# ScalarE instead of SyncE issues attention's plain loads from the second group of heads on

## The chip, the cores and the metric

The kernel runs on one core of a Trainium2 chip. A core has a matrix engine (TensorE, PE in the profile), three engines for elementwise work (VectorE or DVE, ScalarE or ACT, GpSimd or POOL), and SyncE (SP), which does no arithmetic here and issues transfers. Sixteen DMA engines move the data between main memory and the on-chip memory. Each engine takes its own instructions strictly in order, and the engines wait for each other by semaphores. The metric is the device time of one execution in microseconds (us): the median of the runs.

## What is computed

The input x has 1024 rows of 512 numbers. It is normalized by rows, and the result goes into two branches: causal attention with 32 query heads in 8 groups (one key head and one value head for four query heads, each 128 wide) with a linear distance bias, and a feed-forward network with 4-bit weights. The result is x plus the product of the two.

```
xn = layernorm(x)
q, k, v = xn @ Wq.T, xn @ Wk.T, xn @ Wv.T          # 32, 8 and 8 heads of 128
q, k = rmsnorm(q, q_norm_w), rmsnorm(k, k_norm_w)
scores = q @ k.T / sqrt(128) + where(j > i, -1e30, slope[head] * (j - i))
s = concat_heads(softmax(scores) @ v) @ Wo.T
g = silu((silu(xn @ gate) * (xn @ up)) @ down)     # weights (w - zero) * scale
out = x + s * g
```

## The kernel before

The feed-forward network comes first, then the projections of the query, key and value heads, and then attention. Nearly all matrix products use 16-bit numbers in pairs: a value is split into a high and a low half, and one product becomes three matmuls (`mm3`, lines 151 to 153). The feed-forward result (the gates) and the projected heads are parked in main memory: keys in `kd`, values in `vd`, queries in `qd`, gates in `gd`. Attention loads them back, a group of heads at a time.

Attention is a pipeline of 256 steps written out by hand, in `step(n)`. A group of heads has 32 steps: four blocks of 256 query rows (`qb`; from the second group on in the order 2, 3, 0, 1, in the last group 2, 3, 1, 0), and in a block four heads with two tiles of 128 query rows each. A block therefore has 8 steps. Later blocks of rows see more keys (the mask is causal), so their tiles are wider: a tile of block 3 has up to 1024 columns, a tile of block 0 128 or 256. In step n the engines are given, in this order:

- the loads that are due at its start: queries of the next block two steps after a block began, keys of the next group at step 4 of 32, values of the next group at step 24 of 32;
- PE: the scores of step n, into one of two score tiles in PSUM (`s`);
- ACT: every second step, the copy of the finished head outputs of ten steps ago (`heads_hi`, line 1110);
- DVE: the biased scores of step n-1 and their row minimum (line 1041); ACT: their exponentials and row sums (line 1047);
- ACT: the high half of the probabilities of step n-3 (line 1066); DVE: the low half of those of step n-4 (line 1074), and right behind it SP issues a DMA transpose of both halves, from `p16` into `pT` (lines 1082 and 1077);
- PE: the products of probabilities and values of step n-9 (`o`), and between them output projections of an earlier block (`m`), which DVE adds up (line 1149);
- at the step's end, in some steps: loads of gates and x for the last group (`gate_load`), and rows of Wo. Wo's row blocks are loaded at every second step (`load_wo`, line 991), scaled by GpSimd two steps later (line 994), and split into halves two more steps later (lines 1000 and 1001).

Buffers are taken from rings in turn: two slots for keys, values and queries each, four for Wo rows, four for gates, five for `p16`, four for transposed probabilities (two named `pT`, two named `wide`). A transfer into a slot waits until the slot's last reader is done.

All transfers are issued by SP. A DMA transpose goes out on the same queue as the loads, in the order of the program. The queries of the group before the last are transposed as they are loaded (line 962), and those of the last group come from on-chip memory, transposed (line 974).

The first 8 of the 256 steps run between the last projections, and `attention` runs the others. It is in the program twice, once for the case that a bound on the scores allows far keys to be skipped. The branch with the skipping is the one that the profiled execution takes.

Of the kernel before, what the change touches and what calls it, by code (L numbers as in the profile page):

```python
# [22 lines left out]
P = 128  # L23
# [4 lines left out]
NH = 4  # L28
HD = 128
# [7 lines left out]
NQT = QB // P  # L37
# [72 lines left out]
def attention_gated_by_ffn_kernel(ctx, tc, x, gu_w, gu_z, gu_s, dn_w, dn_z, dn_s, wq, wkv, wo, qnw, knw, out):  # L110
    nc = tc.nc
    ve, se, ge, te, sp = nc.vector, nc.scalar, nc.gpsimd, nc.tensor, nc.sync
# [9 lines left out]
    def ps2():  # L122
        return rings["s"].take(F32, 2, 512)
# [52 lines left out]
    kd = [dram.tile([P, 2, NT, 2 * HD], F16, name=f"kd{i}") for i in range(HKV // 2)]  # L176
    vd = [dram.tile([P, NT, 2 * HD], F16, name=f"vd{g}") for g in range(HKV)]
    qd = [dram.tile([NT, P, 2 * NH * HD], F16, name=f"qd{g}") for g in range(HKV)]
    ald = [dram.tile([1, 2 * HD], F32, name=f"ald{i}") for i in range(HKV // 2)]
    gd = dram.tile([NT, P, DM], F32, name="gd")  # L180
# [358 lines left out]
    def finish_step():  # L539

        for f in finishing.pop(clock[0], ()):
            f()
        clock[0] += 1
# [282 lines left out]
    for it in range(NI):  # L826
        for tb in range(2):
# [14 lines left out]
            for i in range(4):  # L842
                c = slice(i * P, i * P + P)
# [100 lines left out]
    NB = S // QB  # L944
    blocks = [(g, qbs) for g in range(HKV) for qbs in (FIRST_ORDER if g == 0 else ORDER if g < HKV - 1 else LAST_ORDER)]
    units = [(g, qb, hh) for g, qbs in blocks for hh in range(NH) for qb in qbs]
    kT, vT, qT, woh, wol = {}, {}, {}, {}, {}
    trel, pT, oT, wor = {}, {}, {}, {}

    def load_keys(g):  # L950
        kT[g] = rings["kT"].take(F16, NT, 2, P)
        sp.dma_start(kT[g].rearrange("p t a k -> p t (a k)"), kd[g // 2][:, g % 2])

    def load_values(g):
        vT[g] = rings["vT"].take(F16, NT, 2, HD)
        sp.dma_start(vT[g].rearrange("p t a d -> p t (a d)"), vd[g])

    def load_queries(g, qb):
        qT[g, qb] = rings["qT"].take(F16, NQT, 2, NH, P)
        if g == HKV - 2:  # L960
            for i in range(NQT):
                sp.dma_start_transpose(qT[g, qb][:, i].rearrange("p a g q -> p (a g) q"), qd[g][qb * NQT + i])
            return
        sp.dma_start(
            qT[g, qb].rearrange("p t a g q -> p t (a g q)"), qd[g][qb * NQT : (qb + 1) * NQT].rearrange("t p c -> p t c")
        )

# [2 lines left out]
    def last_queries(t):  # L970
        g, qb = HKV - 1, t // NQT
        if (g, qb) not in qT:
            qT[g, qb] = rings["qT"].take(F16, NQT, 2, NH, P)
        sp.dma_start_transpose(
            qT[g, qb][:, t % NQT].rearrange("p a g q -> p (a g) q"), last_pairs.pop(t).rearrange("p a g d -> p (a g d)")
        )
# [11 lines left out]

    def load_wo(g, i):
        wor[g, i] = rings["wor"].take(F32, DM)  # L990
        sp.dma_start(wor[g, i], wo[(g * NH + i) * HD : (g * NH + i + 1) * HD, :])

    def scale_wo(g, i):
        ge.tensor_scalar(wor[g, i], wor[g, i], rvs[:, g : g + 1], None, ALU.mult)  # L994
# [8 lines left out]
    def relative(g):  # L1003

        rel = trel[g] = rings["trel"].take(F32, S)
        if g == 0:
            ge.iota(rel, pattern=[[-1, S]], base=S - P, channel_multiplier=1, allow_small_or_imprecise_dtypes=True)
            ge.affine_select(rel, rel, pattern=[[-1, S]], compare_op=ALU.is_ge, fill=1e20, base=S - P, channel_multiplier=1)
            ge.tensor_scalar(rel, rel, rc, float(SLOPES[NH - 1]), ALU.mult, ALU.mult)
        else:  # L1010
            ge.tensor_scalar(rel, trel[g - 1], float(SLOPES[g * NH + NH - 1] / SLOPES[g * NH - 1]), None, ALU.mult)
# [8 lines left out]
    def scores(u, qt):  # L1020
        g, qb, hh = units[u]
        k0 = lowest(u, qt)
        w = (NQT * qb + qt + 1 - k0) * P
        ps = ps2().rearrange("p a c -> p (a c)")
        q = qT[g, qb][:, qt]
        for c0 in range(0, w, 512):
            c1 = min(w, c0 + 512)
            kt = kT[g][:, k0 + c0 // P : k0 + c1 // P]
            mm3(ps[:, c0:c1], (q[:, 0, hh, :], q[:, 1, hh, :]), (kt[:, :, 0, :], kt[:, :, 1, :]), True, True)
        s_ps[u, qt] = ps[:, :w]  # L1030
# [77 lines left out]
    def heads_hi(u):  # L1108
        oh, ol = rings["oh"].take(F16, QB), rings["ol"].take(F16, QB)
        se.activation(oh, av_ps[u], AF.Copy, scale=1.0 / P_SCALE)  # L1110
        oT[units[u]] = (oh, ol)

    def heads_lo(u):
        oh, ol = oT[units[u]]
        ve.scalar_tensor_tensor(ol, av_ps.pop(u), 1.0 / P_SCALE, oh, ALU.mult, ALU.subtract)  # L1115
# [12 lines left out]
    def gate_load(qb):  # L1128
        gx = rings["f"].take(F32, 2, NQT, DM)
        t0 = qb * NQT  # L1130
        sp.dma_start(gx[:, 0], gd[t0 : t0 + NQT].rearrange("t p c -> p t c"))
        sp.dma_start(gx[:, 1], x[t0 * P : (t0 + NQT) * P, :].rearrange("(t p) c -> p t c", p=P))
        gates[qb] = gx

    def gate_partial(qb, i):
# [5 lines left out]
    def accumulate(g, qb, i, other=False):  # L1141
        ps = op_ps.pop((g, qb, i))
        t = qb * NQT + i
        yt = y_rows(t)
        undo = isg[:, g : g + 1]
        if g == 0:
            ve.tensor_scalar(yt, ps, undo, None, ALU.mult)
        elif g < HKV - 1:
            ve.scalar_tensor_tensor(yt, ps, undo, yt, ALU.mult, ALU.add)
        else:  # L1150
            gt = gates[qb][:, 0, i]
            ve.scalar_tensor_tensor(gt, ps, undo, gt, ALU.mult, ALU.mult)
            (ge if other else ve).tensor_tensor(gt, gt, yt, ALU.add)
            sp.dma_start(out[t * P : (t + 1) * P, :], gt)

    order = [(u, qt) for u in range(len(units)) for qt in range(NQT)]
    nn, BS = len(order), NH * NQT
# [3 lines left out]
    for k, (g, qbs) in enumerate(blocks[:-1]):  # L1161
# [5 lines left out]
        n, taken, done = max(free, due), 0, 0  # L1167
        op_first.setdefault(g, n)
        for qb in qbs:
            for i in range(NQT):  # L1170
                for part in range(NH):
# [5 lines left out]
                    if taken == 2 or n < due + done:  # L1177
                        n, taken = n + 1, 0
        free = n + (taken > 0)
    near = [False]  # L1180
    TILES = NT * len(projections)

    def at(n):

        return order[n] if 0 <= n < nn else None
# [3 lines left out]
    def advance(stage, n):  # L1189

        while stages[stage] <= n and at(stages[stage]):
            stage(*at(stages[stage]))
            stages[stage] += 1
# [9 lines left out]
    def step(n):  # L1203
        nonlocal last_ps
        if n < nn:
            u, qt = order[n]
            g, qb, hh = units[u]
            for due in q_at.get(n, ()):
                if due[0] < HKV - 1:
                    load_queries(*due)  # L1210
            for t, due in LAST_QUERIES.items():
                if due == n:
                    last_queries(t)
            if g + 1 < HKV:
                if n % (NB * BS) == KEYS_STEP:
                    relative(g + 1)
                    load_keys(g + 1)
                elif n % (NB * BS) == VALUES_STEP:
                    load_values(g + 1)
            scores(u, qt)  # L1220
        done = at(n - AV_LAG - 1)
        done = done[0] if done and done[1] == NQT - 1 else None
        if done is not None:
            heads_hi(done)
        for stage, lag in ((biased, 1), (exponentials, 1), (split_hi, NQT + 1), (split_lo, NQT + 2)):
            advance(stage, n - lag)
        if done is not None:
            heads_lo(done)
        if n < nn + AV_LAG + 1:
            for due in acc_at.get(n, ()):  # L1230
                accumulate(*due)
        finish_step()

        def project():
            for due in op_at.get(n, ()):
                out_proj(*due)

        if at(n - AV_LAG):
            values(*at(n - AV_LAG), project)
        else:  # L1240
            project()
        if done is not None and units[done][:2] == final:
            g, qb, hh = units[done]
            if hh == 0:
                last_ps = [ps2()[:, 0, :] for i in range(NQT)]
            for i in range(NQT):
                out_proj(g, qb, i, hh)
            if hh == NH - 1:
                for due in acc_at.get(nn + AV_LAG + 1, ()):
                    accumulate(*due, other=True)  # L1250
                for i in range(NQT):
                    accumulate(g, qb, i)
        if n in GATE_LOADS:
            gate_load(LAST_ORDER[GATE_LOADS.index(n)][0])
        for i in range(NQT):
            if n - i in GATE_SUMS:
                gate_partial(LAST_ORDER[GATE_SUMS.index(n - i)][0], i)
        for lead, act in ((WO_SPLIT, split_wo), (WO_SCALE, scale_wo), (WO_LOAD, load_wo)):
            for g, first in op_first.items():
                if n + lead - first in range(0, 2 * NH, 2):  # L1260
                    act(g, (n + lead - first) // 2)
# [36 lines left out]
                early_tile(c)  # L1298

    def attention(only_near):  # L1300
        near[0] = only_near
        for k in range(len(projections) - 2, len(projections)):
            project_all(k)
        for n in range(NT, nn + AV_LAG + 1):
            step(n)

    def frozen():
# [21 lines left out]
    with tc.If(flag > 0) as branch:  # L1329
        attention(True)  # L1330
# [42 lines left out]
```

## Time and profile before

| | |
|---|---|
| median of 3 runs | 1016.7 us (1016.07 to 1020.3) |
| profiled execution | 1020.44 us, span of its instructions 1018.6 us |
| PE busy in the span | 964.7 us (95%) |
| DVE, ACT, POOL busy | 857.2 (84%), 775.5 (76%), 429.4 us (42%) |
| DMA transposes of probabilities | 224 on SP, from 446 us on |
| attention's plain loads on SP | 8 keys, 8 values, 24 queries, 32 rows of Wo, 4 of gates, 4 of x |

The profile is of one execution. A row such as `L1066 ACT ACTIVATE p<-pf,row` is line 1066 of the kernel, on ScalarE, writing the tile `p` from `pf` and `row`. `SPq` and `ACTq` are the queues of SP and ACT themselves: their rows are DMA issues and semaphore waits, which count as no engine's busy time. A DMA row's duration is the time for which the issue held the queue, not the transfer. In the lists of waits, `PE o L151 <- DMA pT<-p: 9.5, 6, 3.7` says that PE, before line 151's matmul into `o`, sat idle 9.5 us in all, in 6 places, the longest 3.7 us, until a DMA from `p` to `pT` had landed. The granted clock is the share of full speed that TensorE was given.

### The profile page before, as it was taken

To read this page: it belongs to the slowest core of one execution; us is meant where nothing else is said; L and a number is where in the kernel's file an instruction comes from. 1 tells how busy PE (TensorE), PEld (TensorE's weight loads), DVE (VectorE), ACT (ScalarE), POOL (GpSimd) and SP (SyncE) were. 2 spreads that over 40 slices of the span, in tenths; PEclk is the share of its full clock that TensorE was granted. 3 is DMA by queue.
4 is the path that set the end of the run, shared out by engine and by line. 5 is a ranking of instruction groups with operands and counts; after the bars stand their busy time and mean duration, and the time that the engine had idled before them with its cause. 6 is when DMAs were issued, how large, how long until landed. Compare 5 with 4: busy or idle time off the path is not lost. (4 is left out here: it accounts for less than half of the span.)

```text
span 1018.6 us, 17980 instructions
## 1 busy us (share of the span) xinstructions
PE 964.7 (95%) x5688; PEld 561.8 (55%) x5688; DVE 857.2 (84%) x1764; ACT 775.5 (76%) x2160; POOL 429.4 (42%) x424
## 2 busy tenths in 40 slices
PE   6899999999999999996998999999999999989995
PEld 4344477854444444444555666665676666656562
DVE  7888998728888878877898998987989989969985
ACT  5777745778878887787887987987879978858861
POOL 2588764216666555564235151051241421530722
PEclk9999999999999999999999999999999999999999
DMA  7132359535998999998898999997999999999994
GB/s 251 37 121 93 104 170 310 187 125 163 204 273 190 245 229 215 236 237 202 172 196 161 206 216 183 227 203 158 231 202 191 212 201 190 202 219 198 218 201 108
DMA packets 425063, 195.74 MB, mean 192 GB/s; under 512 B 371522, under 2 KB 382078, under 8 KB 424958
## 3 DMA queue, kind: packets, MB, share of 16 engines
q1 hardware_dynamic: 424958, 194.50, 85.5%
q8 instruction: 46, 0.75, 0.3%
q14 instruction: 59, 0.48, 0.1%
HBM read 76.27 MB, written 27.27 MB: 102 GB/s over the span
## 5 line engine op out<-in xcount | busy, mean ns | idle before, releaser
L1074 DVE SCALAR_TENSOR_TENSOR p<-pf,row,p 128x384 f16<-128x384 f32 (+7 forms) x256 | 208.8, 816 | 20.9 <-ACT p L1066 18.0
L1047 ACT ACTIVATE pf<-pf,row 128x384 f32<-128x384 f32 (+7 forms) x256 | 184.9, 723 | 41.6 <-DVE row L1041 37.3
L1041 DVE CUSTOM_DVE_ANT_0 pf<-s,trel,cs 128x384 f32<-128x384 f32 (+7 forms) x256 | 191.4, 748 | 19.8 <-PE s L153 19.7
L1066 ACT ACTIVATE p<-pf,row 128x384 f16<-128x384 f32 (+7 forms) x256 | 184.0, 719 | 6.3 <-DMA pT<-p 1.4
L151 PE MATMUL s<-kT,qT 128*128 128x512 f16 (+3 forms) x356 | 115.3, 324 | 11.8 <-DVE row L1041 11.5
L994 POOL TENSOR_SCALAR wl<-wl,rvs 128x512 f32<-128x512 f32 x32 | 53.7, 1677 | 149.0 <-DMA wl<-in_wo 130.0
L152 PE MATMUL s<-kT,qT 128*128 128x512 f16 (+3 forms) x356 | 115.4, 324 | 0.0
L153 PE MATMUL s<-kT,qT 128*128 128x512 f16 (+3 forms) x356 | 114.0, 325 | 0.0
L716 POOL TENSOR_TENSOR f<-f,inv 128x512 f32<-128x512 f32 (+1 forms) x96 | 102.1, 1084 | 1.4
L151 PE MATMUL m<-v,wh 128*128 128x512 f16 x248 | 95.0, 383 | 0.0
L153 PE MATMUL m<-v,wh 128*128 128x512 f16 x248 | 94.9, 383 | 0.0
L151 PE MATMUL o<-pT,vT 128*128 128x256 f16 (+1 forms) x302 | 79.6, 264 | 13.9 <-DMA pT<-p 13.7
L151 PEld LDWEIGHTS <-vT 128*128 128x128 f16 x594 | 58.9, 99 | 57.8 <-DMA pT<-p 15.1
L1110 ACT ACTIVATE wh<-o 128x256 f16<-128x256 f32 x128 | 47.7, 373 | 54.4 <-PE o L153 53.8
L152 PEld LDWEIGHTS <-vT 128*128 128x128 f16 x594 | 58.9, 99 | 41.4 <-issue 4.5
L152 PE MATMUL o<-pT,vT 128*128 128x256 f16 (+1 forms) x302 | 79.6, 264 | 0.0
L153 PE MATMUL o<-pT,vT 128*128 128x256 f16 (+1 forms) x302 | 79.3, 264 | 0.0
L151 PE MATMUL o<-wide,vT 128*128 128x256 f16 (+1 forms) x292 | 75.9, 260 | 3.1 <-DMA wide<-p 3.1
L152 PE MATMUL o<-wide,vT 128*128 128x256 f16 (+1 forms) x292 | 75.9, 260 | 0.0
L153 PE MATMUL o<-wide,vT 128*128 128x256 f16 (+1 forms) x292 | 75.7, 260 | 0.0
L151 PE MATMUL m<-wh,xth 128*128 128x512 f16 x192 | 72.8, 379 | 1.2 <-ACT h L869 1.2
L153 PE MATMUL m<-wh,xtl 128*128 128x512 f16 x192 | 72.8, 379 | 0.0
(200 smaller groups left out, 2531.4 us busy)
## 6 DMA issues: line engine op xcount, KB each, us to landing
qd<-tr SPq DMA_DIRECT2D x48, 256.0 KB, 3.3
qT<-qd SPq DMA_DIRECT2D x24, 512.0 KB, 4.4
wide<-in_wq SPq DMA_DIRECT2D x32, 256.0 KB, 3.7
wo_sq<-in_wo SPq DMA_DIRECT2D x8, 1024.0 KB, 7.8
wl<-in_wo SPq DMA_DIRECT2D x32, 256.0 KB, 3.6
gui<-in_gu_w SPq DMA_DIRECT2D x13, 512.0 KB, 3.7
wide<-in_wkv SPq DMA_DIRECT2D x16, 256.0 KB, 3.8
vd<-v SPq DMA_DIRECT2D x8, 512.0 KB, 4.7
```

The costliest lines, as they stand in the source:

```text
L151: te.matmul(ps, lhsT=lh, rhs=rh, start=first, stop=False)
L152: te.matmul(ps, lhsT=lh, rhs=rl, start=False, stop=False)
L153: te.matmul(ps, lhsT=ll, rhs=rh, start=False, stop=last)
L716: ge.tensor_tensor(f, f, ib, ALU.mult)
L994: ge.tensor_scalar(wor[g, i], wor[g, i], rvs[:, g : g + 1], None, ALU.mult)
L1041: ve.tensor_tensor_reduce(p, ps, trel[g][:, S - w :], cs[:, hh : hh + 1], 3e38, ALU.add, ALU.min, least[:, c])
L1047: se.activation(p, p, AF.Exp, bias=least[:, c], scale=-1.0, accum_out=total[:, c])
L1066: se.activation(p16[u, qt][:, :, 0, :], pf[u, qt], AF.Copy, scale=scale[:, qt : qt + 1])
L1074: ve.scalar_tensor_tensor(lo, p, scale, hi, ALU.mult, ALU.subtract)
L1110: se.activation(oh, av_ps[u], AF.Copy, scale=1.0 / P_SCALE)
```

## The change

From step 32 on (`NB * BS`, where the second group of heads begins), the plain loads of keys, values, queries, Wo rows, gates and x are issued by ScalarE's queue (`se`) and no longer by SyncE's (`sp`). They stand at the same places of the program, and what they load, from where and to which buffer is the same. The transposes, those of the queries among them, and the output's stores stay on SyncE. The loads of the first group's steps, up to step 31, stay there too.

```diff
+    def loads():
+        return se if loads_by_act[0] else sp
+
     def load_keys(g):
         kT[g] = rings["kT"].take(F16, NT, 2, P)
-        sp.dma_start(kT[g].rearrange("p t a k -> p t (a k)"), kd[g // 2][:, g % 2])
+        loads().dma_start(kT[g].rearrange("p t a k -> p t (a k)"), kd[g // 2][:, g % 2])
     def load_values(g):
         vT[g] = rings["vT"].take(F16, NT, 2, HD)
-        sp.dma_start(vT[g].rearrange("p t a d -> p t (a d)"), vd[g])
+        loads().dma_start(vT[g].rearrange("p t a d -> p t (a d)"), vd[g])
...
@@ load_queries, the plain form
-        sp.dma_start(
+        loads().dma_start(
             qT[g, qb].rearrange("p t a g q -> p t (a g q)"), qd[g][qb * NQT : (qb + 1) * NQT].rearrange("t p c -> p t c")
         )
...
@@ load_wo
-        sp.dma_start(wor[g, i], wo[(g * NH + i) * HD : (g * NH + i + 1) * HD, :])
+        loads().dma_start(wor[g, i], wo[(g * NH + i) * HD : (g * NH + i + 1) * HD, :])
...
@@ gate_load
-        sp.dma_start(gx[:, 0], gd[t0 : t0 + NQT].rearrange("t p c -> p t c"))
-        sp.dma_start(gx[:, 1], x[t0 * P : (t0 + NQT) * P, :].rearrange("(t p) c -> p t c", p=P))
+        loads().dma_start(gx[:, 0], gd[t0 : t0 + NQT].rearrange("t p c -> p t c"))
+        loads().dma_start(gx[:, 1], x[t0 * P : (t0 + NQT) * P, :].rearrange("(t p) c -> p t c", p=P))
...
-    near = [False]
+    near, loads_by_act = [False], [False]
...
     def attention(only_near):
-        near[0] = only_near
+        near[0], loads_by_act[0] = only_near, False
         for k in range(len(projections) - 2, len(projections)):
             project_all(k)
         for n in range(NT, nn + AV_LAG + 1):
+            loads_by_act[0] = n >= NB * BS
             step(n)
```

## The prediction, made before the change was run

> **What bounds the kernel now.** I read the waits first, cut to the stretch in which the change acts. The second group's first moved load is issued at 511 us, and the last at 989, so I ask for 515 to 1000 us: who waited, for whom, how long, how often, the longest.
>
> ```profile
> PE o L151 <- DMA pT<-p: 9.5, 6, 3.7
> PE s L151 <- DVE row L1041: 6.0, 4, 2.5
> PE o L151 <- DMA wide<-p: 3.1, 3, 2.3
> ```
>
> The matrix engine (PE) idles about 19 us in 485: 12.6 us until a DMA transpose of probabilities (pT or wide) has landed, 6.0 us until VectorE has freed a score bank. The rest is matmul work that this change leaves alone. So an improvement must come out of the transposes' lateness, and it has a ceiling. The same stretch by windows (microseconds, then busy PE, weight loads, VectorE, ScalarE, GpSimd; granted clock; DMA share; GB/s):
>
> ```profile
> 645.00:716.00 71.00, 68.97 (x476) 44.09 (x474) 61.98 (x139) 57.26 (x132) 18.61 (x14) 0.98 1.01 195
> ...
> 850.00:920.00 70.00, 64.02 (x439) 40.57 (x438) 57.16 (x125) 52.51 (x122) 22.23 (x18) 0.98 1.04 213
> 920.00:960.00 40.00, 37.91 (x245) 23.11 (x243) 39.69 (x69) 31.89 (x60) 17.21 (x10) 0.96 1.09 206
> ...
> sum 485.00, PE 465.43 PEld 297.23 DVE 434.46 ACT 391.09 POOL 151.14; mean PE 58.18 PEld 37.15 DVE 54.31 ACT 48.89 POOL 18.89
> ```
>
> ScalarE (ACT) is busy 391 of 485 us (81%), VectorE 434 (90%). ACT has 94 us free in total, but not everywhere. The DMA share near 1 warns that the transfers may be limited by the DMA engines and not by who issues them. Finer windows around one stall, same columns:
>
> ```profile
> 676.00:684.00 8.00, 8.00 (x70) 6.17 (x68) 7.65 (x21) 5.33 (x18) 3.93 (x6) 1.00 1.23 216
> 684.00:688.00 4.00, 1.97 (x18) 1.45 (x17) 2.17 (x9) 2.24 (x8) 0.31 (x1) 1.00 0.92 195
> 688.00:692.00 4.00, 4.00 (x19) 2.33 (x17) 1.08 (x4) 0.00 (x0) 0.00 (x0) 0.57 0.64 166
> ```
>
> PE loses 2.03 us idle, and in the next 4 us it is granted 0.57 of its clock: 4 x 0.43 = 1.7 us more. A stall costs nearly twice its idle time. SyncE's queue before it:
>
> ```profile
> 668.68 1.12 SPq L991 DMA_DIRECT2D wl<-in_wo  x1
> 669.90 2.98 SPq L1082 DMA_TRANSPOSE wide<-p  x1
> 672.99 4.31 SPq L1082 DMA_TRANSPOSE pT<-p  x2
> 677.39 0.72 SPq L964 DMA_DIRECT2D qT<-qd  x1
> 678.21 6.41 SPq L1082 DMA_TRANSPOSE pT<-p  x2
> ```
>
> SyncE (SP) goes from one issue to the next with 0.1 us between. The two transposes for which PE waits stand behind a query load that holds SP 0.72 us, and behind a Wo row (1.12 us). From 651.6 to 678.1 us four Wo rows and two query loads take 0.97+0.90+0.77+0.89+1.12+0.72 = 5.4 us of SP.
>
> **The change, part by part.** *What leaves SP.* Sixty-seven issues: 28 Wo rows, 19 query loads, 6 keys, 6 values, 4 gates, 4 rows of x. By their medians on SP (0.822, 0.580, 0.574, 0.575, 0.581, 0.476 us) they hold it 23.0+11.0+3.4+3.5+2.3+1.9 = 45 us; with 0.1 us between issues, 52. What remains on SP are the transposes: 84 at 1.475, 84 at 1.426, 14 at 1.241, 13 at 1.233, and 16 of queries near 1.27, so 297 us by medians, and the output stores. SP goes from some 0.72 of the stretch to 0.61.
>
> *What that is worth.* At the 684 us stall the last two transposes could start up to 0.8 us sooner (the query load), and more if SP had not lagged before. The stalls at 889 and 895 us have transposes of queries in front, which stay on SP. So I take half of the 12.6 us: 6.3. The clock row adds (1 - 0.98) x 71 + (1 - 0.98) x 70 = 2.8 us in the two windows with such stalls; half is 1.4. Gain 7.7 us; the bounds are 0 (the DMA engines set the landing) and 12.6 + 2.8 = 15.4.
>
> *What ACT takes on.* No row shows ACT issuing a DMA; its price is bounded by SP's rows, 0.40 us (shortest Wo row of the whole trace) to 1.46 (longest key load); I take SP's 0.58, nearest because the transfers are the same. That is 67 x 0.58 = 39 us of ACT's queue. How much holds up its arithmetic? One line's view in a window of 2.4 us shows ACT's queue ahead of its engine:
>
> ```profile
> L1066 ACTq EVENT_SEMAPHORE  x1: 17/17/17, 656.2 to 656.2; - x1
> L1066 ACT ACTIVATE p<-pf,row x1: 1042/1042/1042, 657.7 to 657.7; 128x896 f16<-128x896 f32 x1
> ```
>
> The queue's semaphore instruction runs at 656.2, 1.5 us before the split it belongs to, while the exponential before that split starts only at 656.49. A queue instruction thus runs once the waits ahead of it are met, not once the arithmetic ahead is done. A load is covered by arithmetic already released. The 28 Wo rows come at the end of a step, behind an exponential and a split (medians 0.721 and 0.705 us): 0.58 + 0.1 lies under 1.43, cost 0. Queries, keys and values (31) stand behind a split that waits for the row scale: 0.68 against 0.705, cost about 0. The gate pairs (4) are 0.58 + 0.48 + 0.2 = 1.26 against 0.705: 0.55 each, 2.2 us. On the path I charge 1.5, since ACT has idle time in each window. Bounds: 0, and, with nothing covered, 67 x 0.68 = 46 less whatever of the 94 us idle absorbs it.
>
> *New waits.* What is queued behind a load on ACT are the heads' copies, exponentials and splits; VectorE's low halves wait for those, SP's transposes for these, PE for the transposes. But the buffers are free by then: a query slot's last scores come three steps before the load, and ACT has already run the exponential of a later step's scores; keys four steps, values sixteen, Wo rows most of a group later. Cost 0, with that order as the cover; if an earlier DMA's landing is waited for instead, at most a landing, 3.6 us for Wo rows, beyond what ran meanwhile. GpSimd issues no DMA and only gets Wo rows earlier: its 118 us of waiting for them is idle time that nobody needs.
>
> *Sum.* -7.7 + 1.5 = -6.2 us. The profiled execution took 1020.4 us (span 1018.6 and 1.8 around it), so 1014.2 of its kind; it stands 3.7 above the median of the runs, 1016.7, so 1010.5.
>
> **Two rules against it.** The row: 297 us of transposes in 485, and a DMA share of 1.01 to 1.23. The Trainium skill (DMA: Bandwidth & Descriptors, "Issuing engines are not separate DMA queues") says that DMAs from any engine run on the same 16 engines, and that a second issuer saves only sequencer time, usually small. Taken strictly, the term of 7.7 is only SP's part: at the 684 us stall 0.8 us of 2.03. It would bring about 3 us.
> Its page Perfetto Trace Analysis, "DMA Instruction — HWDGE (DVE, Sync)", has the descriptor generator locked for exclusive use during an issue. No row here shows two issuers. If so, ACT's loads queue behind SP's transposes, and by that rule SP wins nothing; the sum becomes that of the third rival.
>
> **Rivals.** *One: hidden anyway.* For it: the DMA share, and the two transposes at 678 take 6.41 us where the two before them take 4.31: what slows an issue that far is transfers, not SP. A load of 512 KB moves over the same engines whoever issues it. Against it: the 0.1 us spacing, SP really queues. Time: 0 to -3 from freed SP time, +1.5: 1016.
>
> *Two: all late transposes catch up.* The ceiling, 15.4 us, with no ACT cost: 1001. Against it: the query transposes that remain.
>
> *Three, slower: ACT is held by SP's transposes.* Place: a load at ACT's step start that must wait until SP's running transpose is issued. SP transposes 297/485 = 61% of the time, with some 1.4 us each; a chance arrival waits 0.61 x 0.7 = 0.43 us on average, and under the long ones of 2 to 4 us far more. An issue of 1.2 us plus 0.1 exceeds the 0.705 cover by 0.6: 35 x 0.6 = 21 us of ACT, in stretches where VectorE follows ACT closely (VectorE waited 14.8 us for ACT's splits, 45 times). If half reaches PE, +10.5, with no gain: 1027. It decides once ACT's loads take over about 1.1 us at the median. For it: direct loads on SP take up to 1.46 us just behind transposes. Against it: most are near 0.58, the wait there could be SP's own queue.
>
> That the change does nothing is no rival: the branch taken uses these very lines (the loads are in the trace).
>
> **How the numbers follow.** A difference under 0.5% (5 us) is about what a measurement of this kernel can't tell from none. Forecast (-5 to -10): 0.32, point 1010.5. Hidden (within 5 us): 0.30. Full catch-up (-10 to -16): 0.08. Held ACT (above +5): 0.30. So faster 0.40, same 0.30, slower 0.30. The range runs from the ceiling, 1001, to 1027, leaving out 2 in 10, mostly above; the forecast's own range is 1006 to 1012.
>
> **What would show it.** Right: loads appear in ACT's queue at about 0.6 us, PE's waits for pT and wide fall from 12.6 toward 6 us, fewer windows show a clock below 1, ACT's waits are unchanged. Hidden: PE's waits stay, transposes on SP as long as before. Held: ACT's loads above 1.1 us, VectorE's waits for ACT's splits well above 14.8 us, PE's waits for VectorE's row above 6.0. Wrong altogether: if ACT's queue can't run ahead past a load, or if a load waits there for a buffer or an earlier DMA, each would pass its whole length on to the exponentials.

## The result and the profile after

The changed kernel takes 1026.5 us (median of 8 runs, 1023.0 to 1030.6); the kernel before takes 1017.7 us in the same comparison (8 runs, 1014.7 to 1023.6). The ratio is 1.0089, 95% interval 1.0068 to 1.0109: slower by 0.9%, or 8.8 us. The direction forecast was wrong. The profiled execution of the changed kernel took 1023.75 us (span 1022.0, mean granted clock 0.985; before 1020.44, 1018.6 and 0.989), which is 2.8 below the median of its kind, as that of before was 2.7 above. The two traces therefore differ by only 3.4 us of span, and I read them for places, not for the sum.

The waits of the changed kernel, of PE alone, from 515 to 1000 us (us in all, places, the longest):

```profile
PE o L151 <- DMA pT<-p: 15.8, 9, 4.8
PE s L151 <- DVE row L1045: 6.7, 9, 1.3
```

Before, PE waited 9.5 + 3.1 = 12.6 us for transposes; now it waits 15.8. The wait that was to shrink has grown. The wait for VectorE's row (6.0 before) is nearly as it was. From 515 to 1000 us the clock takes no more than before: the mean granted clock there is 0.987 after and 0.986 before, which is 6.3 and 6.8 us lost. The difference between the two traces in this stretch is idle time.

The issues of the moved loads, from the views of their six lines in the changed kernel (count, then shortest, median and longest ns, first and last start):

```profile
L956 ACTq DMA_DIRECT2D kT<-kd x6: 330/338/364, 515.7 to 848.9; - x6
...
L960 ACTq DMA_DIRECT2D vT<-vd x6: 333/346/393, 555.0 to 897.1; - x6
...
L968 ACTq DMA_DIRECT2D qT<-qd x19: 377/383/402, 512.6 to 815.5; - x19
...
L995 ACTq DMA_DIRECT2D wl<-in_wo x28: 334/344/399, 523.7 to 955.8; - x28
...
L1135 ACTq DMA_DIRECT2D f<-gd x4: 372/383/384, 887.6 to 988.4; - x4
...
L1136 ACTq DMA_DIRECT2D f<-in_x x4: 503/553/984, 888.0 to 988.9; - x4
```

The change does what it says, and an issue on ACT is short: 0.34 to 0.55 us by the medians of its six lines, with one of 0.98. ScalarE is busy as before (775.9 us against 775.5), and VectorE waits no longer for ACT's high halves (14.6 us against 14.8). Nobody is held up by ACT.

The page's DMA queues, after (packets, MB, share of the 16 engines' time):

```profile
q1 hardware_dynamic: 411854, 166.71, 76.0%
q10 hardware_dynamic: 13104, 27.79, 9.4%
```

and before:

```profile
q1 hardware_dynamic: 424958, 194.50, 85.5%
```

The loads have become a queue of their own, q10. The packets' time is the same in sum (85.4% against 85.5%). Last, the time from issue to landing, from the views of the tile `pT` and then of `wide` between 511 and 1000 us, before (shortest, median, longest):

```profile
DMA to landing us min/median/max: 2.7/4.1/6.3
...
DMA to landing us min/median/max: 2.7/4.0/7.7
```

and after:

```profile
DMA to landing us min/median/max: 2.7/4.4/7.4
...
DMA to landing us min/median/max: 2.8/4.1/8.8
```

So SP was relieved, and the transposes were no better off. For the 115 transposes (114 after) whose landing the traces hold from step 32 on, I took the differences of three times: the end of the low half that a transpose waits for, its issue, its landing. The mean from low half to issue fell from 1.03 to 0.81 us; the mean from issue to landing rose from 4.13 to 4.42. Together 5.16 before and 5.23 after: what was won at the issue was lost in flight. These are the transposes whose landing the views give; some slow ones, the one of 8.19 us below among them, are left out. With the last completion record of each taken as its landing, all of them in this stretch can be counted: from issue to landing 4.13 us before (197) and 4.56 after (198), and over 7 us took 1 before and 12 after.

**The place where it shows.** In the third group of heads, SP's queue before (start, us held, what):

```profile
606.01 1.61 SPq L1082 DMA_TRANSPOSE pT<-p  x1
607.72 1.03 SPq L964 DMA_DIRECT2D qT<-qd  x1
608.85 6.72 SPq L1082 DMA_TRANSPOSE pT<-p  x2
```

A transpose goes out first, then the query load of the next block (512 KB), then the next transposes. PE did not wait for any of these: from 606 to 618 us it waits only for VectorE:

```profile
PE s L151 <- DVE row L1041: 0.7, 1, 0.7
```

The same place in the changed kernel, SP's queue, then ACT's:

```profile
607.08 9.95 SPq L1086 DMA_TRANSPOSE pT<-p  x3
```

```profile
607.14 0.39 ACTq L968 DMA_DIRECT2D qT<-qd  x1
```

The load now leaves in the same instant as that first transpose, 0.06 us behind it, instead of 1.7 us. The chain of the changed kernel through this stretch (start, us, what):

```profile
606.30 0.21 PE m L151
...
607.08 8.19 DMA pT<-p
615.27 0.05 issue
615.32 0.38 PE o L151
...
617.41 0.43 PE m L151
```

The transpose takes 8.19 us to land (before, the same one, issued at 606.01, took 5.5 by its last completion record), and PE, which needs it, idles 1.5 us until it has (PE's waits from 606 to 619 us):

```profile
PE o L151 <- DMA pT<-p: 1.5, 1, 1.5
PE s L151 <- DVE row L1045: 0.7, 1, 0.7
```

The trace's packet records show the order in flight. The transposes here move packets of 256 bytes, the query load packets of 2048. Before, from 607.6 to 610.6 us, the load has been issued, but all packets under 512 bytes are the transposes', and the only other one is an instruction fetch:

```profile
DMA packets 1492, 0.40 MB, mean 133 GB/s; under 512 B 1491, under 2 KB 1491, under 8 KB 1491
```

After, from 609.0 to 610.2 us, there are packets of the load alone:

```profile
DMA packets 175, 0.36 MB, mean 299 GB/s; under 512 B 0, under 2 KB 0, under 8 KB 175
q10 hardware_dynamic: 175, 0.36, 84.4%
```

The packets of the transpose issued at 607.08 start behind them, 3.2 us after its issue; before, they had started within 1.8. The load, issued 0.06 us later than the transpose, went ahead of it.

Then the clock drops: the windows of the same kernel (us, then busy PE, weight loads, VectorE, ScalarE, GpSimd; granted clock; DMA share; GB/s):

```profile
606.00:611.00 5.00, 5.00 (x44) 3.62 (x43) 4.54 (x10) 4.87 (x13) 3.84 (x3) 1.00 0.98 221
611.00:615.40 4.40, 2.16 (x19) 1.34 (x18) 4.08 (x11) 2.65 (x12) 2.73 (x5) 1.00 1.28 139
615.40:618.80 3.40, 3.40 (x14) 1.90 (x15) 0.55 (x4) 1.09 (x4) 0.59 (x2) 0.50 1.09 243
```

For 3.4 us the granted clock is 0.50, and the matmul `m` of line 151, 0.21 us in the chain at 606.30, takes 0.43. Half of 3.4 us is another 1.7 us lost. Idle and clock make up 3.2 us, and the block of eight steps around it grew by 3.1.

### The profile page after: what moved, and what is told of

It reads as the page before. It is cut to its first block, busy times and chain, and to the rows that moved or that the text cites. A ratio compares the mean times of both kernels' runs of the same rounds, so it can differ in the third digit from the quotient of the medians.

```text
span 1022.0 us, 17989 instructions
## 1 busy us (share of the span) xinstructions
PE 965.1 (94%) x5688; PEld 562.0 (55%) x5688; DVE 857.5 (84%) x1764; ACT 775.9 (76%) x2160; POOL 428.3 (42%) x424
## 4 chain that ended last, share of the span: by engine, by line
PE 71%; DMA 9%; DVE 8%; ACT 5%; issue 4%; POOL 3%; SPq 0%; DVEq 0%; POOLq 0%; ACTq 0%
PE o L151 8%; PE o L152 8%; PE o L153 8%; PE m L151 8%; PE m L152 8%; PE m L153 8%; DMA pT<-p 7%; PE gu_ps L326 6%; PE s L151 4%; PE s L153 4%; PE s L152 4%; PE dn_ps L151 1%; PE dn_ps L153 1%; PE dn_ps L152 1%; ACT p L1070 1%
## 5 line engine op out<-in xcount | busy, mean ns | idle before, releaser
L1078 DVE SCALAR_TENSOR_TENSOR p<-pf,row,p 128x384 f16<-128x384 f32 (+7 forms) x256 | 207.1, 809 | 22.3 <-ACT p L1070 19.0
L1045 DVE CUSTOM_DVE_ANT_0 pf<-s,trel,cs 128x384 f32<-128x384 f32 (+7 forms) x256 | 191.4, 748 | 19.2 <-PE s L153 19.1
L152 PE MATMUL m<-wl,xth 128*128 128x512 f16 x192 | 72.8, 379 | 0.0
```

What stands on the lines that cost most here:

```text
L152: te.matmul(ps, lhsT=lh, rhs=rl, start=False, stop=False)
L1045: ve.tensor_tensor_reduce(p, ps, trel[g][:, S - w :], cs[:, hh : hh + 1], 3e38, ALU.add, ALU.min, least[:, c])
L1078: ve.scalar_tensor_tensor(lo, p, scale, hi, ALU.mult, ALU.subtract)
```

## The experiments

A block below is one of eight steps, from the start of its first biased scores (line 1041 before, 1045 after) to that of the next block, both from the trace. Three stretches vary with the loads and are given for every run: the third block of the third group (steps 80 to 87), the third block of the seventh group (steps 208 to 215), and the tail, from the last block's start to the end. They come from one profiled execution of each kernel, so their spread counts: in the runs that leave the loads near a stretch as before, the third group's block takes 15.7 to 16.0 us, the seventh's 22.2 to 23.5, the tail 38.9 to 40.2. The ratios come from 6 to 12 runs of each, against the kernel before on the same chip.

| run | ratio to before, 95% interval | third group | seventh group | tail |
|---|---|---|---|---|
| before | 1 | 15.8 | 23.5 | 39.1 |
| the change | 1.0089 (1.0068 to 1.0109) | 18.9 | 25.0 | 40.7 |
| tiny_on_act | 0.9995 (0.9976 to 1.0013) | 15.6 | 21.5 | 39.1 |
| wo_on_act | 0.9991 (0.9972 to 1.0010) | 15.9 | 21.8 | 39.0 |
| thin_sp | 0.9930 (0.9911 to 0.9949) | 15.6 | 19.5 | 39.2 |
| thin_act | 0.9991 (0.9974 to 1.0008) | 15.5 | 24.0 | 40.4 |
| gates_on_act | 1.0057 (1.0031 to 1.0082) | 16.0 | 23.5 | 42.0 |
| rest_on_act | 1.0047 (1.0028 to 1.0066) | 19.0 | 24.9 | 39.0 |
| first_gates_215 | 1.0109 (1.0083 to 1.0135) | 19.3 | 20.5 | 39.8 |
| gates_207_sp | 1.0024 (1.0003 to 1.0045) | 15.9 | 26.1 | 39.2 |
| queries_lead1_sp | 1.0023 (1.0005 to 1.0040) | 19.0 | 22.3 | 38.9 |
| safe_on_act | 0.9997 (0.9975 to 1.0019) | 19.2 | 17.8 | 38.8 |
| gates_early_sp | 1.0025 (1.0008 to 1.0041) | 15.8 | 23.4 | 40.2 |
| wo_gates_early_sp | 0.9998 (0.9981 to 1.0014) | 15.8 | 22.3 | 38.6 |
| one_query_on_act | 1.0032 (1.0015 to 1.0050) | 19.6 | 23.4 | 39.4 |
| values_on_act | 1.0035 (1.0019 to 1.0050) | 15.7 | 25.5 | 39.3 |
| last_gates_on_act | 1.0025 (1.0006 to 1.0044) | 15.8 | 22.2 | 41.8 |
| safer_on_act | 1.0017 (0.9995 to 1.0038) | 15.6 | 19.5 | 38.3 |

**Is it ACT?** *tiny_on_act* keeps all loads on SP and lets ACT issue 67 extra loads of 128 x 4 bytes at the same places.

```diff
+        if loads_by_act[0]:
+            se.dma_start(tiny[:, c : c + 1], x[:P, c : c + 1])
+        return sp
```

> All loads stay on SyncE; at each of the 67 places ScalarE issues in addition a load of 128 x 4 bytes into a scratch tile that nobody reads. The contention theory (loads on a second queue run beside the transposes and make them land later) expects no slowdown, because hardly a byte moves: 1016 to 1019 us against about 1017.7 before. The issue theory (each issue of 0.34 us on ScalarE's queue delays the exponentials, and they PE) expects the whole loss: about 1026 us, since the queue is held as often as in the changed kernel.

Measured 1018.6 us, ratio 0.9995. Sixty-seven issues on ACT (0.335 us in the median) cost nothing that can be measured, so the loss is not ScalarE's time.

**Is it the bytes?** *thin_sp* and *thin_act* load an eighth of the bytes of each key, value, query and Wo load, on SP and on ACT; gates and x stay whole. These two kernels leave out data, so only their times mean anything.

```diff
+        c = to.shape[-1] // 8
+        return to[..., :c], of[..., :c]
...
-        sp.dma_start(vT[g].rearrange("p t a d -> p t (a d)"), vd[g])
+        sp.dma_start(*thin(vT[g].rearrange("p t a d -> p t (a d)"), vd[g]))
```

> SyncE issues all loads, and from the second group on each load moves an eighth of its bytes (the rest of the buffer keeps older data, and Wo rows are scaled by 1 instead of the group's factor, so the result is not the reference's). Partner of the next kernel. If the loads' bytes are what makes the transposes late before the change, PE's waits for transposes fall well below 12.6 us and the time falls by 5 to 15 us; if it is SyncE's issue time, the time stays within 3 us of before.

> As the kernel before it, but ScalarE issues the loads from the second group on, as in the changed kernel. Contention theory: with an eighth of the bytes the second queue can't hurt; equal to the partner, or up to 5 us faster through SyncE's freed queue. Issue theory: slower than the partner by the same 9 us as the changed kernel against before.

Measured 1011.2 and 1018.8 us. On SP seven eighths of the bytes of these 59 loads are worth 0.7%, and PE's waits for transposes (515 to 1000 us) fall from 12.6 to 6.4 us: bytes matter before the change too. On ACT the third group's block is back at 15.5 us: a thin query load on ACT does no harm, so it is the bytes in flight beside the transpose that do. But thin_act still lost 7.6 us to thin_sp, where equal or faster was expected, with the whole gate and x loads the only large ones on ACT. That pointed at single loads, which the next runs took apart.

**Which loads?** *wo_on_act* moves the 28 Wo rows alone, *gates_on_act* the eight loads of gates and x alone, *rest_on_act* all but these eight. Each is the change with some `loads()` put back to `sp`:

```diff
 # gates_on_act: keys, values, queries and Wo back on SP
-        loads().dma_start(wor[g, i], wo[(g * NH + i) * HD : (g * NH + i + 1) * HD, :])
+        sp.dma_start(wor[g, i], wo[(g * NH + i) * HD : (g * NH + i + 1) * HD, :])
```

> Only the 28 Wo rows go to ScalarE; queries, keys, values and gates stay on SyncE. Contention theory: in proportion to bytes, 7.3 of 27.8 MB, some +2.5 us. Issue theory: in proportion to count, 28 of 67, +3.8 us, or nothing if these issues are covered by the exponential and split ahead of them, as the prediction had it.

> Only the 8 gate and x loads go to ScalarE. Overtaking theory (SyncE lags some 10 us behind ScalarE's place in the program where block 3 of a group ends; there ScalarE issues the first gate pair, 1 MB that is needed only later, ahead of transposes that PE is about to wait for): the whole loss of the changed kernel, 1024 to 1028 us, and block 0 of the seventh group 24 us or longer. General contention, in proportion to bytes: 4.2 of 27.8 MB, some +1.4 us.

> The other 59 loads (keys, values, queries, Wo rows) go to ScalarE, gates and x stay on SyncE. Overtaking theory: no loss, 1012 to 1019 us, because these loads are issued near the time at which SyncE issued them. General contention: most of the loss, some +7.6 us, 1025.

Measured 1018.2, 1025.5 and 1024.1 us. The Wo rows, 42% of the moved issues, do no harm. Eight gate and x loads cost 0.57%; in the profiled execution they lengthen the tail by 2.9 us and the third block of the eighth group from 19.1 to 21.0. The rest costs 0.47%, in the third and the seventh group, and leaves the tail alone. The two add up to 1.04%, the whole change to 0.89%, equal within the intervals. Two expectations failed here: the gates were to hold the whole loss and to lengthen the seventh group's block (it stayed at 23.5), and the rest was to cost nothing.

**Does another step cure the gates?** *first_gates_215* is the change with the first gate pair four steps later; *gates_207_sp* is the kernel before with that pair four steps earlier.

```diff
-GATE_LOADS = [211, 219, 235, 251]
+GATE_LOADS = [215, 219, 235, 251]   # first_gates_215; gates_207_sp has 207
```

> The changed kernel, with the first of the four gate pairs loaded at step 215 instead of 211, about 9 us later and so about when SyncE used to issue it. Overtaking theory: block 0 of the seventh group shrinks from 25 to 21 to 23 us, and the time by 3 to 5 us, to 1022. If the engine that issues is what costs, no change: 1026.

> The kernel before, ScalarE issues nothing; the first gate pair is moved four steps forward, to step 207, so that SyncE issues it ahead of the last four wide transposes of that block instead of behind them. Overtaking theory: the same stall as in the changed kernel without any change of engine, +3 to +6 us, 1021 to 1024. If the engine or the second queue is the cause: no change, about 1018.

Measured 1031.0 and 1021.5 us. Four steps later did not help, where 3 to 5 us less was expected: the seventh group's third block fell to 20.5 us, but its fourth rose from 14.4 to 19.7. Four steps earlier on SP put the pair ahead of more transposes, and that block became the longest of all runs, 26.1 us; the time rose by 0.24%, some 2.4 us, a little less than the 3 to 6 expected. SP gives no protection by itself; what counts is what stands behind the load.

**Order, without ACT.** *queries_lead1_sp* leaves every load on SP and issues the query loads one step sooner in their blocks, so that each stands ahead of the transpose behind which it stood.

```diff
-        for qb, lead in zip(blocks[k + 1][1], (6, 10) if steps > BS else (2, 5)):
+        for qb, lead in zip(blocks[k + 1][1], (6, 10) if steps > BS else (1, 5)):
```

> No load is on ACT here; SP issues the query loads of a group's first block one step of heads earlier than before, so that they stand ahead of the transpose behind which they stood. Order theory (a load harms when it moves beside or ahead of a transpose that PE needs next, whoever issues it): the third group's first block of queries grows from 15.8 toward 19 us with a PE stall of over 1 us in it, and the time is up by 2 to 6 us, 1020 to 1025. Engine theory (the loss belongs to ACT as issuer, or to two rings at once): no change, within 1.5 us, the block stays at 15.8.

Measured 1019.6 us, ratio 1.0023. SP's queue in this run, then its chain, then PE's own row with its idle time in brackets:

```profile
606.15 1.03 SPq L964 DMA_DIRECT2D qT<-qd  x1
607.28 7.00 SPq L1082 DMA_TRANSPOSE pT<-p  x2
```

```profile
607.28 7.63 DMA pT<-p
```

```profile
614.95 0.28 PE L151 MATMUL o<-pT,vT 128*128 128x256 f16 x1 [1.62 <-DMA pT<-p]
```

The block takes 19.0 us, as with the load on ACT (18.9 to 19.6 in the six runs where it stood beside or ahead of the transpose at its full size, counting this one), and not 15.8. From 609.0 to 610.2 us the packets are the load's alone here too (175, none under 512 bytes). The same stall comes from the order alone, with one queue and one issuer. This is what decides, at this place, between the order and the engine; for the gates gates_207_sp speaks to the same question, and for the values no run does.

**One load at a time.** *one_query_on_act* has a single load of the 67 on ACT, the query load shown above. *values_on_act* has the six value loads there, *last_gates_on_act* the last pair of gates and x.

```diff
 # one_query_on_act
-        sp.dma_start(
+        (loads() if (g, qb) == (2, 1) else sp).dma_start(
             qT[g, qb].rearrange("p t a g q -> p t (a g q)"), ...
```

```diff
 # last_gates_on_act: only gate_load uses loads(), and
+            loads_by_act[0] = n == GATE_LOADS[-1]
```

> One load of the 67 on ACT, the third group's last query load (512 KB), all else on SP. Order theory: the third group's block that holds it grows from 15.8 to about 19 us with a PE stall of 1.5 to 1.9 us, no other block differs, time up by 2 to 4 us, 1020 to 1022, ratio 1.002 to 1.004. If the loss needs the whole stream on the second ring: no change of that block, ratio within 0.0015 of 1.

> Only the six value loads (512 KB each) on ACT. Order theory: the seventh group's first block of small rows grows to 24 to 25.5 us (21.5 to 23.5 before), with a PE wait of 4.5 to 5 us for the transpose issued beside the load; the other groups unchanged, time up by 1 to 3 us, ratio 1.001 to 1.003. If values are harmless: ratio within 0.0015 of 1 and the block at most 23.5.

> Two loads on ACT, the last pair of gates and x, which go out just ahead of a late transpose of the last group. Order theory: the tail, from the last block of steps to the end, grows from 39.1 to between 40.5 and 42 us with a PE wait of over 3 us for that transpose, time up by 1.5 to 3 us, ratio 1.0015 to 1.003. If not: tail 38.9 to 39.3 and ratio within 0.001 of 1.

Measured 1.0032, 1.0035 and 1.0025, each with an interval above 1. The chain and PE's waits (608 to 620 us) of one_query_on_act:

```profile
609.74 9.11 DMA pT<-p
```

```profile
PE o L151 <- DMA pT<-p: 2.4, 1, 2.4
```

In values_on_act the value load goes out 2.2 us behind the transposes' issue, beside them; ACT's queue, the chain, and PE's waits from 880 to 920 us:

```profile
897.23 0.33 ACTq L960 DMA_DIRECT2D vT<-vd  x1
```

```profile
895.04 7.50 DMA pT<-p
```

```profile
PE o L151 <- DMA pT<-p: 7.6, 2, 6.0
```

and the same chain and waits in the kernel before, where the values wait behind four transposes, until 902.43:

```profile
893.54 5.48 DMA pT<-p
```

```profile
PE o L151 <- DMA pT<-p: 5.5, 2, 3.7
PE o L151 <- DMA wide<-p: 0.5, 1, 0.5
```

The transpose lands 7.50 us after its issue instead of 5.48, and PE's longest wait grows from 3.7 to 6.0. In last_gates_on_act, ACT's queue, SP's queue and the chain:

```profile
985.18 0.39 ACTq L1135 DMA_DIRECT2D f<-gd  x1
985.62 0.59 ACTq L1136 DMA_DIRECT2D f<-in_x  x1
```

```profile
985.99 1.23 SPq L1086 DMA_TRANSPOSE pT<-p  x1
```

```profile
985.99 7.53 DMA pT<-p
```

Here the loads leave 0.4 to 0.8 us ahead of the transpose, which takes 7.53 us, and PE waits 3.4 us for it; the tail is 41.8 us instead of 39.1. From 986.0 to 989.7 us 465 of the 466 packets are those of the loads, and the transpose's start after them. Before, the same pair went out right behind that transpose, which landed 3.1 us after its issue. Nine loads of 67 account for 0.32 + 0.35 + 0.25 = 0.92%, against 0.89% for the change. The agreement is partly luck: each term is known to about 0.2%, and the other three gate pairs (0.57 - 0.25 = 0.32%, by difference) are not in this sum. The first of them goes out in the block of the seventh group that the values burden as well, so the prices need not add.

**Can the good part be kept?** *safe_on_act* leaves on ACT the Wo rows, the keys and the queries of all blocks of rows but block 0.

```diff
-        loads().dma_start(vT[g].rearrange("p t a d -> p t (a d)"), vd[g])
+        sp.dma_start(vT[g].rearrange("p t a d -> p t (a d)"), vd[g])
...
+        (loads() if qb else sp).dma_start(
```

> On ACT from the second group on: Wo rows, keys and the queries of each block but a group's first; values, the first blocks' queries, gates and x stay on SP. Most of the moved issues, but none that my traces show in front of a late transpose. Order theory: no loss, ratio 0.997 to 1.002, third group's first block 15.8 us, seventh group's first block at most 23.5, tail 39.1. If instead any heavy load on a second ring slows transposes in proportion to its bytes: about three fifths of the loss of the whole change, +5 us, 1023.

Measured 1017.4 us, ratio 0.9997, as the order theory had it, but not for its reason. I had put the wrong query loads back: the harmful one of the third group belongs to block 1 of rows, and stayed on ACT. The chain there is as bad as in the change,

```profile
608.66 8.26 DMA pT<-p
```

and the block took 19.2 us, not 15.8. What made up for it in this execution was the seventh group's block, 17.8 us, with PE's waits from 880 to 920 us at

```profile
PE o L151 <- DMA pT<-p: 1.6, 1, 1.6
PE o L151 <- DMA wide<-p: 1.5, 1, 1.5
```

instead of 5.5 and 0.5. That is 3 us less waiting, and the clock did not drop there; it suggests that a lighter SP queue can help as the prediction hoped, where the loads that left it don't come back beside the same transposes. No run takes this apart. *safer_on_act* was to keep that and put the harmful query load back on SP:

```diff
-        (loads() if qb else sp).dma_start(
+        (loads() if qb > 1 else sp).dma_start(
```

> As the run with Wo, keys and most queries on ACT, but the last query load of each group, which stood beside a late transpose, is back on SP too. Order theory: the third group's block back at 15.8 us (19.2 there) and the rest kept, so 2 to 4 us less than that run: 1013.5 to 1016 against 1017.6 before, ratio 0.996 to 0.999. If that block was not the price of that load: ratio as in that run, 0.9997 within 0.0015.

Measured 1.0017 (0.9995 to 1.0038): the block is back at 15.6 us, as expected, but the time isn't lower. A stall stood in the second group, with a query load on ACT 0.7 us behind a transpose that also followed a value load on SP; the chain there:

```profile
555.73 1.04 SPq L960
...
556.88 8.53 DMA pT<-p
```

PE idled 2.1 us after it, and that block took 16.1 us where safe_on_act had 13.8. Yet safe_on_act has the same transfers in the same order there; its transpose landed in 7.1 us, PE waited 0.8, and the clock stayed at 1. The profiled execution was nevertheless quick, 1016.8 us where the median is 1022.0, so its blocks don't explain the median of this run. Why safer_on_act isn't faster stays open.

**Can the bytes be moved away on SP?** *gates_early_sp* loads the first three gate pairs 49 to 89 steps earlier, in the last blocks of the fourth to sixth groups; *wo_gates_early_sp* also loads the Wo rows 12 steps earlier.

```diff
-GATE_LOADS = [211, 219, 235, 251]
+GATE_LOADS = [122, 154, 186, 251]
...
+                early = 12 if act is load_wo and g else 0   # wo_gates_early_sp only
```

> All on SP; the first three pairs of gate and x loads are issued at steps 122, 154 and 186, in the second block of queries of three earlier groups, instead of 211, 219 and 235 in the seventh and eighth group. If the bytes of the gate pairs beside the query transposes are part of the seventh group's stall: its first block falls from 23.5 toward 19.5 to 21.5 us and the time by 2 to 4 us, 1013 to 1015 against 1017. If the stall is set by the query transposes alone: no change, within 1.5 us.

> As the run with the early gate pairs, all on SP, and the Wo rows from the second group on are issued 12 steps earlier as well, so that they no longer fall beside the next group's first transposes. If bytes ahead of late transposes are what costs: 4 to 8 us less than before, 1010 to 1013. If SP's order alone shields the transposes already: as the run with the early gates alone, within 1.5 us. If the Wo rows meet other transposes there: slower than that run by up to 4 us.

Measured 1.0025 and 0.9998; both expected gains failed. The seventh group's block kept its 23.4 us without any gate load in it. So on SP the gate pair was no part of that stall: it stood behind the transposes that PE waited for. The failure thus fits the order theory and refutes only my guess about the seventh group. Why gates_early_sp is 0.25% slower isn't settled; its tail was 40.2 us. No version that beats the kernel before came out of these runs.

## Why the prediction was wrong, step by step

- **What bounds the kernel: right.** PE's idle time comes mostly from late transposes. That a stall costs nearly twice its idle time holds only where the clock drops after it, as in the third group: 1.5 us idle, then 3.4 us at 0.50. Over the whole stretch before, 18.6 us of idle time stand beside 6.8 us lost to the clock. The Trainium skill (TensorE: Matmul & The Clock Gate, "Part 1: The HAM clock gate (the "warmup" mystery)") gives the gate two states, half and full clock, and a window of about 3.4 us; the drop here agrees, 0.50 for 3.4 us.
- **"What leaves SP", and "What that is worth": the step that failed.** SP's issues did come sooner, 0.22 us in the mean. The term of -7.7 us took each gain at the issue to be a gain at the landing, and its lower bound was 0, "the DMA engines set the landing". That bound left out a loss. In SP's queue the query load's packets came after those of the transpose issued ahead of it; on its own queue they went first. In flight the transposes lost 0.29 us in the mean (0.43 with all of them counted), and three that PE needed next took 8.19, 7.38 and 7.30 us (issued at 607.08, 884.65 and 989.26) where the median is 4.4. The term measured about +8.8 us, since no other term of the sum differs from zero. The stall at 684 us, on which the term leaned, was also larger in that one execution than in others: in last_gates_on_act and gates_207_sp, whose program is that of before up to there, PE waited 1.3 and 1.6 us in its place instead of 2.0, and the clock stayed at 1.00 instead of 0.57.
- **ACT's price: too high, and harmless.** 0.58 us was taken, 0.34 to 0.55 us measured. The 1.5 us on the path measured -0.5 us with tiny_on_act, zero within its interval.
- **ACT's queue runs ahead: right,** and it did the harm. The query load started at 607.14 us together with the split that stands before it in ACT's order (607.13). A load that leaves promptly leaves early, beside or ahead of the transpose of the same step.
- **New waits, "cost 0": right for ACT** (VectorE's wait for it 14.6 us, before 14.8); but the step asked only who is queued behind the load on its new engine. It should also have asked who was queued ahead of it on the old one, and would no longer be.
- **The rule on issuing engines** (the Trainium skill, DMA: Bandwidth & Descriptors, "Issuing engines are not separate DMA queues") was taken as a limit on the gain. The trace agrees that the same 16 engines carry the load: packet time 85.4% against 85.5%. The same page, "Queues, rings and completion order", says that each DMA engine takes turns, packet by packet, between the queues for which it has work. By it a load on a second queue need not follow the transpose. I had not drawn on this, and it speaks against the change. The trace shows the outcome, the load's packets ahead of the transpose's in the third group and 8.19 us to landing instead of 5.5. Whether each engine took turns it doesn't show, since its packet records don't name the engine.
- **Rival three** had the sign and a price near the result (1027), but not the mechanism: it needed issues above 1.1 us, and the medians are below 0.56. A wait for the descriptor generator's lock doesn't show: ACT issued in 0.39 us at 607.14, inside SP's transposes from 607.08 on, and the 53 of its 67 issues that begin while SP issues take 0.35 us in the median, the other 14 take 0.38. The page (the Trainium skill, Perfetto Trace Analysis, "DMA Instruction — HWDGE (DVE, Sync)") names VectorE and SyncE as sharing the generator, and notes that which two engines issue such transfers is the compiler's choice. I had taken the lock to last for a whole issue, and these rows don't bear that out.
- **Rivals one and two** fell: the transposes were neither caught up nor indifferent.
- **The range** held the result, at its upper end, for a reason that none of its cases had. That is luck.

## What to carry over

A shared queue is also an order: before a transfer is given its own queue, list what it stood behind, and ask whether somebody waits for those. Here large loads did less harm right behind the urgent small transfers of a step, and one 512 KB load moved beside a single late one cost 0.3%. When an issuer is relieved, measure the landing and not the issue.

## What was not expected of the hardware

A load on a second queue slowed even transposes issued before it: in values_on_act it came 2.2 us later, and the transpose still took 7.50 us instead of 5.48. Its packets had all started by 899.5 us there, before most of the load's; what held its end back until 902.5 is not shown. A plain load's issue took ACT 0.34 us in the median where SP, among transposes, took 0.57 for a key load and 0.82 for a Wo row. And a late transpose need not cost anything: in the fifth and sixth groups of the changed kernel the same query load stood beside the same transpose, which landed 6.7 and 6.8 us after its issue (before 4.8 and 4.9), and PE didn't wait for it; in the third group, at 8.2 us, it idled 1.5 us and the clock dropped as well. What the same wait costs varies too: with the last pair of gates and x on ACT, PE's longest wait in the tail is 3.2 to 3.4 us in five executions (the change, thin_act, gates_on_act, first_gates_215, last_gates_on_act), but the clock then stayed up in one of them, dropped to 0.50 for 3.4 us in two and for 6.8 us in two; their tails are 39.8, 40.4 and 40.7, and 41.8 and 42.0 us.
